# A conditioned two-stage block on one core: three bias matmuls, the order of the opening's loads and the order of VectorE's statistics are changed

## The chip, the cores and the metric

One of the eight NeuronCores of a Trainium2 chip (trn2) runs the kernel. The metric is device time in microseconds (us) of one launch. All arithmetic that matters here is float32; every float32 matmul goes through TensorE in two passes, which is why the profile counts two instructions for each matmul of the program.

## The reference

x is 32 batches of 128 tokens with 512 features; `cond` is 32 x 512; the mask is 32 x 128.

```python
emb = silu(t) @ ada_w + ada_b
shift, scale, gate_msa = split(emb, 3, axis=1)
norm = layernorm(x) * (1 + scale[:, None]) + shift[:, None]
norm = where(mask, norm, 0)
ssm_out = where(mask, (gelu(norm @ ssm_w1 + ssm_b1) @ ssm_w2 + ssm_b2)
                    + (gelu(norm @ bwd_w1 + bwd_b1) @ bwd_w2 + bwd_b2), 0)
x = x + gate_msa[:, None] * ssm_out
ff_ada = silu(t) @ ffada_w + ffada_b
shift, scale, gate = split(ff_ada, 3, axis=1)
ff_norm = layernorm(x) * (1 + scale[:, None]) + shift[:, None]
return x + gate[:, None] * (gelu_tanh(ff_norm @ ff_w1 + ff_b1) @ ff_w2 + ff_b2)
```

The first stage has an effect on masked tokens alone. The mask of these inputs marks the tail of a batch, up to 32 tokens.

## The kernel before

**Two stages.** The first stage gathers the masked tokens into 512 *slots*, four tiles of 128 (`xc[0]` to `xc[3]`). The slots' token numbers are counted from the mask with small matmuls (`slots_to_count`, L254) and compares on VectorE (`counted`). Tiles 0 and 1 are called early, tiles 2 and 3 late. Each tile is normalised, scaled and shifted (`modulated_by_strips`, L347 and L351), transposed by TensorE (`transposed_slots`, L193), copied by ScalarE (L196) and multiplied with `w1` (`hidden_of_tile` L673, `hidden` L204) and `w2` (`project`, L221). The result goes to DRAM (`x1_wide`, `x1_rows`), from where indirect gathers put the rows back in their places among the straight rows of x (`take_first_rows`, L813). The second stage runs over four pairs of two groups of four batches, and multiplies by a 7-product (Strassen) scheme: `FirstProduct` (L1118) and `SecondProduct` (L1305).

**Conditioning.** `mod1` (first stage) and `mod2` (second stage) hold shift, scale and gate. Matmuls of the transposed silu(cond) with `ada_a` or `ada_f` (`modulation_matmuls`, L309) add up in a PSUM bank. Before them the bank is filled with the bias by a matmul of `quarter`, a widened 4 x 4 identity, with `modb`, the bias rows (`modulation_bias`, L296). There are three such banks: `pm_ss` (shift and scale of stage one), `pm_g` (its gate) and `pm_f` (all three of stage two). VectorE copies each bank to SBUF (`modulation_rows`, L320). `of_slots` (L333) spreads the rows of `mod1` over the slots of a tile. The spread rows in PSUM are called strips (`part_s0` for tiles 0 and 1 together, `part_s2` for tiles 2 and 3).

**Order.** Almost everything stands under a manual schedule: each engine runs its instructions in the order of the program's text, and waits only on semaphores. All large loads go through SyncE's queue (SP), in order. They are, after `ada_a`'s first two thirds: `w1`'s first half (behind a one-element memset by GpSimd that holds it back until the first gather is issued), `ada_a`'s gate third, `w1`'s second half, `raw[0]`, `raw[1]`, `b2`, `b2b`, `w2`'s first half, `fw1` (2 MB), `w2`'s second half, `raw[2]`, `raw[3]`, `ada_f` (3 MB). `raw[n]` are the first eight batches of x, two in each tile of 512 KB.

**VectorE's order in the first stage**, after the early slots: the gate's rows; the statistics of `raw[0]` and `raw[1]` (`own_statistics`, L171), those of both late tiles, the strips of late tile 2, `b2 + b2b` (L792), the strips of late tile 3; the four combinations of `fw1` (`Weights.combine`, L394); the statistics of `raw[2]`; `finish_slots(0)` (L372 on), which ends with the store to `x1_wide`; the statistics of `raw[3]`; `weight_sums(3)` (L733); `finish_slots(1)`; the rows of `mod2` (L320); the normalised rows of the first four batches (L842), whose gathers read `x1_wide`.

On TensorE, the transposes of `mod2` (`ptr_mod`, L866) stand between the first and the second block of the late tiles' hidden layer, and everything behind them waits for `mod2`.

In the first pair (p == 0), at the change from the first to the second product, VectorE normalises and turns the rows of the next pair (`blocks(0, i)`, L929 and L1476) between the sums that the second product reads (`first_block`, L1252). When all four are turned, SP moves them with 16 transfers into `xT` (`to_feature_rows`, L956), ScalarE scales them (L939) and VectorE forms the sums of the next product (L986).

`keep_clock` (L620), L647 and `on_zeros` (L453) are matmuls whose result nobody reads.

Of the kernel before, what the change touches and what calls it, by code (L numbers as in the profile page):

```python
# [9 lines left out]
F32 = mybir.dt.float32  # L10
# [12 lines left out]
def kernel(  # L23
# [49 lines left out]
    nc = tc.nc  # L73
# [55 lines left out]
    def load_conditioning_bias(at, vec, queue):  # L129
        queue.dma_start(modb[at], vec.rearrange("(m j c) -> j m c", m=3, c=P))  # L130

    def load_blocks(t, w):
        nc.sync.dma_start(t, w.rearrange("(k p) f -> p k f", p=P))

    def load_behind_gathers(t, w):
        nc.gpsimd.memset(t[0:1, 0, 0:1], 0.0)
        load_blocks(t, w)

    modb = adap.tile([B + KC, 3, P], F32, name="modb")
    AT_A, AT_F = slice(0, KC), slice(B, B + KC)  # L140
    load_conditioning_bias(AT_A, ada_b, nc.sync)
# [47 lines left out]
    def transposed_slots(xn, dst, name):  # L189

        ptr = ps_t.tile([P, 512], F32, tag="tr", name=f"ptr_{name}")
        for k in range(KC):
            nc.tensor.transpose(ptr[:, ts(k, P)], xn[:, ts(k, P)], ident)  # L193
        for half_no in range(2):
            k = ts(half_no, KC // 2)
            nc.scalar.copy(dst[:, k], ptr.rearrange("p (k s) -> p k s", s=P)[:, k])  # L196
# [53 lines left out]
    def slots_to_count(picked, n, name, bank):  # L250

        pl = bank[0].tile([P, 512], F32, tag=bank[1], name=f"pl_{name}")
        for c in range(n):
            nc.tensor.matmul(pl[:, ts(c, S)], picked[:B, ts(c, P)], rank, start=True, stop=True)  # L254
        return pl[:, : n * S].rearrange("p (c s) -> p c s", s=S)
# [20 lines left out]
    def gather(dst, token_col):  # L276
        nc.gpsimd.indirect_dma_start(
            out=dst,
            out_offset=None,
            in_=x_rows,  # L280
            in_offset=bass.IndirectOffsetOnAxis(ap=token_col, axis=0),
        )
# [6 lines left out]
    def gather_slots(token_i):  # L289
        both = xp.tile([P, 2, D], F32, tag="x", name=f"xc_{len(xc)}")  # L290
        for c in range(NC // 2):
            gather(both[:, c], token_i[:, c : c + 1])
            xc.append(both[:, c])

    def modulation_bias(pm, at, lo, hi):
        nc.tensor.matmul(  # L296
            pm[:, : (hi - lo) * P],
            quarter[at],
            modb[at, lo:hi],
            start=True,  # L300
            stop=True,
            skip_group_check=True,
        )

    def modulation_matmuls(pm, ada, lo, hi, blocks):
        kinds = ada.rearrange("p k (m d) -> p k m d", d=D)
        for k in blocks:
            for j in range(KC):
                nc.tensor.matmul(  # L309
                    pm[ts(j, B), : (hi - lo) * P],  # L310
                    sT[:, k, :],
                    kinds[:, k, lo:hi, ts(j, P)],
                    start=False,
                    stop=True,
                    skip_group_check=True,
                )

    def modulation_rows(pm, mod, lo, hi):
        view = pm[:, : (hi - lo) * P].rearrange("p (m c) -> p m c", c=P)
        nc.vector.tensor_copy(mod[:, lo:hi], view)  # L320
# [130 lines left out]
    def on_zeros(*widths):  # L451
        for n in widths:
            nc.tensor.matmul(pm_keep_clock[:, :n], zeros[:, :P], zeros[:, :n], start=True, stop=True)  # L453
# [69 lines left out]
    def one_more_scale(at):  # L523
        nc.gpsimd.tensor_scalar(modb[at, 1], modb[at, 1], 1.0, None, ALU.add)

    one_more_scale(AT_A)
# [43 lines left out]
    quarter = adap.tile([B + KC, P], F32, name="quarter")  # L570
    for at in (AT_A, AT_F):
        nc.scalar.copy(
            quarter[at].rearrange("p (j b) -> p j b", b=B), ident[at, at].unsqueeze(2).to_broadcast([KC, KC, B])
        )
# [7 lines left out]
    load_conditioning_bias(AT_F, ffada_b, nc.scalar)  # L582

    both = xp.tile([P, 2, D], F32, tag="x", name="xc_0")
    for c, bank in enumerate(((ps_o, "o"), (ps_t, "tr"))):
        if c:
            on_zeros(256)
        slot = slot_col[:, c : c + 1]
        token_c = tokens_of(pick[:, ts(c, P)], slot, 1, f"s0_{c}", ssm, bank)
        xc.append(both[:, c])  # L590
        gather(xc[c], token_c)
        if c == 0:
            load_behind_gathers(w1[:, :, :D], ssm_w1)
    load_behind_gathers(ada_a[:, :, 2 * D :], ada_w[:, 2 * D :])
    load_blocks(w1[:, :, D:], bwd_w1)
    raw = [x_tile(2 * n, 2) for n in range(2 * G // 2)]
# [30 lines left out]

    pm = ps_o.tile([P, 512], F32, tag="o", name="pm_ss")
    modulation_bias(pm, AT_A, 0, 2)
    modulation_matmuls(pm, ada_a, 0, 2, range(KC))  # L630
    slots_of_late = slots_to_count(pick[:, NH:], NC // 2, "s1", (ps_h, "h"))
    modulation_rows(pm, mod1, 0, 2)

    strips = of_slots(pick, (0, 1), mod1, slice(0, 2), 3 * [(ps_o, "o")] + [(ps_h, "h")], "part_s0")
    keep_clock(2, 0)
# [4 lines left out]
    for c in range(2):  # L640
        mv, rstd = statistics(xc[c : c + 1], f"s{c}")
        xn_s.append(
            modulated_by_strips(xc[c], strips, c, xn[:, c], mv[:, 0, 0:1], rstd, xn[:, 2 + c])
        )
        if c == 0:
            for n in range(2):
                nc.tensor.matmul(  # L647
                    pm_keep_clock[:, ts(n, 2 * P)], ident, xn[:, 2, ts(n, 2 * P)], start=True, stop=True
                )
            token_i = counted(slots_of_late, slot_col[:, NC // 2 :], NC // 2, "s1", ssm)  # L650
    gather_slots(token_i)
    one_more_scale(AT_F)
# [4 lines left out]
    fb2 = const.tile([P, D], F32, name="fb2")  # L657
    load_blocks(fw1, ff_w1)
    load_blocks(w2[:, KC:], bwd_w2)
# [22 lines left out]
    transposed_slots(xn_s[0], xT_s[:, :, ts(0, P)], "s0")  # L682
# [10 lines left out]
    modulation_bias(pm, AT_A, 2, 3)  # L693
    modulation_matmuls(pm, ada_a, 2, 3, range(KC))
    modulation_rows(pm, mod1, 2, 3)
# [82 lines left out]
    for n in range(2):  # L778
        own_statistics(raw[n], 2, f"x_{n}")
    mv_t, rstd_t = statistics(xc[2:], "s23")  # L780
# [4 lines left out]
    for c in range(2):  # L785
        xn_late.append(
            modulated_by_strips(
                xc[2 + c], strips, c, spare[1][:, c], mv_t[:, c, 0:1], rstd_t[:, c : c + 1]
            )
        )  # L790
        if c == 0:
            nc.vector.tensor_tensor(b2, b2, b2b, ALU.add)  # L792
# [7 lines left out]
    own_statistics(raw[2], 2, "x_2")  # L800
# [31 lines left out]
    modulation_bias(pm, AT_F, 0, 3)  # L832
# [21 lines left out]
    modulation_rows(pm, mod2, 0, 3)  # L854
# [574 lines left out]
    for p in range(NP):  # L1429
# [78 lines left out]
        if more_pairs:  # L1508
            blocks(0, 2)
        second.step(1, late=True)  # L1510
        now.do(4, "P4")
        if more_pairs:
            blocks(0, 3)
            to_feature_rows(0, nc.sync)
        second.load_gate(1)
        second.first_block(1, 0, 2)
        second.seed_and_second_block(0)
# [172 lines left out]
```

## Time and profile before

| | us |
|---|---|
| three timed runs | 454.81, 454.75, 453.96 (median 454.75) |
| the profiled execution's own time | 454.21 |
| its span on the core | 452.5 |
| TensorE busy | 445.4 (98%) |
| VectorE busy | 334.2 (74%) |
| ScalarE busy | 178.5 (39%) |
| GpSimd busy | 158.0 (35%) |

The profile is of one execution on the chip. Times count from the start of the span. PE is TensorE, PEld its weight loads, DVE VectorE, ACT ScalarE, POOL GpSimd, SP SyncE; SPq marks a DMA issue. "L296" is line 296 of the kernel before. In the timeline a line has start, duration, engine, line, operation, output and input, how many are merged, and in brackets the idle time of the engine ahead of it and what ended it. In the chain of work a line has start, length and what. The chain gives each instruction the time from the end of its predecessor, the timeline its full duration.

### The profile page before, as it was taken

The page shows a single profiled execution, that of the slowest core. Times are in us where ns is not written, and L with a number is a line of the kernel's source. Part 1 is how long each engine was busy: PE and PEld are TensorE (multiplying, and loading weights), DVE is VectorE, ACT ScalarE, POOL GpSimd, SP SyncE. Part 2 cuts the span into 40 slices and gives each one's busy share as a digit, 9 for nine tenths or more (in the row PEclk, how much of TensorE's full clock was granted, in tenths as well). Part 3 has the DMA queues.
Part 4 walks back from the last instruction along what each step waited for, and adds up shares of the span by engine and source line. Part 5 has one row for each costly group of instructions (what it writes and reads, how often), then busy time and mean ns, then how long its engine had stood idle before and what let it go on. Part 6 is the DMA issues. An engine that isn't in the chain of part 4 may idle for free.

```text
span 452.5 us, 6201 instructions
## 1 busy us (share of the span) xinstructions
PE 445.4 (98%) x2151; PEld 370.6 (82%) x2151; DVE 334.2 (74%) x571; ACT 178.5 (39%) x390; POOL 158.0 (35%) x154
## 2 busy tenths in 40 slices
PE   8999999999999999999999999999999999999995
PEld 3885585688888888888888888888888888888884
DVE  5798797877799759987895598868964995434645
ACT  3124127253642551546425524464255144642000
POOL 4220550089770000797700007977000027560000
PEclk9999999999999999999999999999999999999999
DMA  7999449757327817741277177412771434122022
GB/s 254 376 395 408 152 72 332 246 186 236 123 98 159 115 49 257 245 138 36 89 172 112 48 251 245 141 38 90 167 106 58 175 128 129 35 94 93 0 92 98
DMA packets 84916, 70.58 MB, mean 156 GB/s; under 512 B 63368, under 2 KB 63984, under 8 KB 83858
## 3 DMA queue, kind: packets, MB, share of 16 engines
q1 hardware_dynamic: 70066, 58.28, 42.0%
q0 software_dynamic: 4160, 10.54, 6.8%
q10 hardware_dynamic: 10656, 1.33, 2.1%
q8 instruction: 18, 0.29, 0.3%
q14 instruction: 16, 0.13, 0.1%
HBM read 56.46 MB, written 13.70 MB: 155 GB/s over the span
## 4 chain that ended last, share of the span: by engine, by line
PE 94%; DVE 3%; POOL 1%; ACT 1%; issue 1%
PE a_o L1305 22%; PE a_m L1118 20%; PE e_o L1305 18%; PE e_m L1118 15%; PE po_s L221 6%; PE ph_s L204 5%; PE ph_s L673 2%; PE pm_ss L309 1%; PE last L1305 1%; PE a_m_alone L1118 1%; PE pm_f L309 1%; DVE s L1252 1%; PE pl_s L254 1%; PE part_s L333 0%; DVE xn L929 0%
## 5 line engine op out<-in xcount | busy, mean ns | idle before, releaser
L1169 POOL TENSOR_TENSOR ha<-p_m,ha 128x512 f32<-128x512 f32 x20 | 25.8, 1291 | 179.6 <-ACT ha L1176 169.7
L1305 PE MATMUL e_o<-fw,ha 128*128 128x256 f32 x256 | 57.9, 379 | 0.0
L939 ACT ACTIVATE xT<-xT,modT 128x128 f32<-128x128 f32 x112 | 44.2, 480 | 31.8 <-DMA xT<-xn 30.2
L1305 PE MATMUL a_o<-t,hb 128*128 128x256 f32 x240 | 54.1, 379 | 0.0
L1305 PEld LDWEIGHTS e_o<-fw,ha 128*128 128x128 f32 x256 | 48.6, 190 | 6.6
L1305 PEld LDWEIGHTS a_o<-t,hb 128*128 128x128 f32 x240 | 45.6, 190 | 6.2
L1080 ACT ACTIVATE hb<-hb,biasT 128x256 f32<-128x256 f32 x64 | 29.0, 500 | 29.5 <-POOL hb L1202 16.1
L1132 ACT COPY p_m<-e_m 128x512 f32<-128x512 f32 x27 | 15.8, 586 | 48.3 <-PE e_m L1118 44.2
L1305 PE MATMUL e_o<-fw,s 128*128 128x256 f32 x128 | 29.0, 380 | 0.6 <-DVE s L1252 0.6
L885 POOL DMA_INDIRECT x<-x_rows,slot_i x24 | 27.2, 1135 | 6.2 <-issue 5.4
L1169 POOL TENSOR_TENSOR hb<-p_m,hb 128x512 f32<-128x512 f32 x20 | 29.2, 1458 | 0.3
L1305 PE MATMUL a_o<-fw,ha 128*128 128x256 f32 x128 | 28.9, 379 | 0.0
L1305 PE MATMUL a_o<-t,s 128*128 128x256 f32 x128 | 28.9, 379 | 0.0
L221 PE MATMUL po_s<-w,h_s 128*128 128x512 f32 x64 | 28.4, 594 | 0.0
L1176 ACT COPY ha<-e_m 128x512 f32<-128x512 f32 x32 | 18.6, 580 | 24.8 <-PE e_m L1118 20.6
L1305 PEld LDWEIGHTS e_o<-fw,s 128*128 128x128 f32 x128 | 24.2, 190 | 4.3 <-DVE s L1252 1.0
L1305 PEld LDWEIGHTS a_o<-fw,ha 128*128 128x128 f32 x128 | 24.3, 190 | 3.3
L1305 PEld LDWEIGHTS a_o<-t,s 128*128 128x128 f32 x128 | 24.3, 190 | 3.3
L1143 DVE TENSOR_TENSOR e_m<-a_m,ha 128x512 f32<-128x512 f32 x20 | 14.0, 698 | 17.0 <-POOL ha L1169 7.6
L1080 ACT ACTIVATE ha<-e_m,biasT 128x256 f32<-128x256 f32 x48 | 20.1, 469 | 14.4 <-PE e_m L1118 14.2
L1118 PE MATMUL a_m<-xT,tw 128*128 128x256 f32 x96 | 24.7, 380 | 0.0
L1118 PE MATMUL e_m<-s,fw 128*128 128x256 f32 x92 | 23.7, 380 | 0.0
(237 smaller groups left out, 895.0 us busy)
## 6 DMA issues: line engine op xcount, KB each, us to landing
x<-in_x_dram SPq DMA_DIRECT2D x16, 512.0 KB
tw<-t_rows SPq DMA_DIRECT2D x16, 512.0 KB
gate<-gate_rows POOLq DMA_DIRECT2D x8, 1024.0 KB
out_dram<-x SPq DMA_DIRECT2D x15, 512.0 KB
tw<-t_rows SPq DMA_DIRECT2D x16, 384.0 KB
xT<-xn SPq DMA_DIRECT2D x92, 64.0 KB
ada_f<-in_L_cond_ffada_w_dram SPq DMA_DIRECT2D x4, 768.0 KB
ada_a<-in_L_cond_ada_w_dram SPq DMA_DIRECT2D x4, 512.0 KB
```

The source lines that it names most:

```text
L204: nc.tensor.matmul(ph[:, :n], w[:, k, ts(f, P)], xT[:, k, :], start=(k == 0), stop=(k == KC - 1))
L221: nc.tensor.matmul(po, h[f][:, ts(i, P)], w[:, f, :], start=(f == 0 and seeded is None), stop=(f == HC - 1), skip_group_check=seeded is no ...
L309: nc.tensor.matmul(pm[ts(j, B), : (hi - lo) * P], sT[:, k, :], kinds[:, k, lo:hi, ts(j, P)], start=False, stop=True, skip_group_check=True,)
L885: nc.gpsimd.indirect_dma_start(out=xs[i // G][i % G // 2][:, i % 2], out_offset=None, in_=x1_rows, in_offset=bass.IndirectOffsetOnAxis(ap= ...
L939: nc.scalar.activation(out, src, AF.Identity, bias=shift, scale=scale)
L1080: nc.scalar.activation(dst[:, n], src[:, n], AF.Gelu_apprx_tanh, bias=biasT[:, f : f + 1])
L1118: nc.tensor.matmul(bank[:, ts(n, QT)], self.w_block(j, product)[:, ts(n, P)], self.x_block(j, product), start=(product in ("P1", "P5") and ...
L1132: nc.scalar.copy(p5, e)
L1143: nc.vector.tensor_tensor(e, a, p5, add)
L1169: nc.gpsimd.tensor_tensor(self.place(RESULT[j], c), self.p5[j], other, ALU.add)
L1176: nc.scalar.copy(self.place(RESULT[j], c), src)
L1305: nc.tensor.matmul(part, src[:, k, ts(i, P)], w[product][:, k, :], start=(last and k == 0), stop=True, skip_group_check=True,)
```

## The change

1. The bias of the gate and of the second conditioning is no longer a matmul. It is loaded in broadcast form (each bias row to 32 partitions, 512 bytes a piece: `ada_b`'s gate part on SP behind `w1`'s second half, all of `ffada_b` on SP behind `ada_f` instead of on ScalarE's queue), and added by VectorE when it takes the rows out of PSUM: one `tensor_tensor`, and for the scale a `scalar_tensor_tensor` that also adds the 1.
2. The bias of `pm_ss` stays a matmul, but stands ahead of the second counting matmul, in place of a filler. ScalarE instead of VectorE copies `pm_ss` out.
3. In the opening, tile 0's strips are made alone (4 matmuls instead of 8) and tile 1's after tile 0's transposes. The second late counting matmul goes behind tile 0's strips. Fillers are halved. Tile 0's transposes go to two PSUM banks, so that ScalarE's first copy can start after two of them.
4. The gather of late tile 2 is issued ahead of tile 1's statistics, the one of tile 3 right behind them.
5. `ssm_w1` is loaded in two column halves (1 KB instead of 2 KB a piece). `w2`'s second half goes ahead of `fw1` on SP.
6. VectorE's order: `raw[0]`, then late tile 2 whole, late tile 3 whole, `b2 + b2b`, `raw[1]`, `raw[2]`, and only then the combinations of `fw1`.
7. In the first pair, `blocks(0, 2)` and `blocks(0, 3)` with the transfers to `xT` move behind `second.load_gate(1)`, the one around and the other behind `first_block(1, 0, 2)`.

```diff
-    def load_conditioning_bias(at, vec, queue):
-        queue.dma_start(modb[at], vec.rearrange("(m j c) -> j m c", m=3, c=P))
+    def load_conditioning_bias(t, vec, kinds):
+        rows = vec.rearrange("(m j c) -> m j c", m=3, c=P)
+        for n, m in enumerate(kinds):
+            nc.sync.dma_start(t[:, n], rows[m].unsqueeze(1).to_broadcast([KC, B, P]))
...
-    def transposed_slots(xn, dst, name):
+    def transposed_slots(xn, dst, name, apart=False):
+        ptr = [ps_t.tile([P, 512], F32, tag="tr", name=f"ptr_{name}")]
+        if apart:
+            ptr.append(ps_t.tile([P, 512], F32, tag="tr", name=f"ptr_{name}_1"))
...
-    def modulation_rows(pm, mod, lo, hi):
+    def modulation_rows(pm, mod, lo, hi, bias=None):
         view = pm[:, : (hi - lo) * P].rearrange("p (m c) -> p m c", c=P)
-        nc.vector.tensor_copy(mod[:, lo:hi], view)
+        if bias is None:
+            nc.vector.tensor_copy(mod[:, lo:hi], view)
+            return
+        other = slice(0, hi - lo, 2)
+        nc.vector.tensor_tensor(mod[:, lo:hi][:, other], view[:, other], bias[:, other], ALU.add)
+        if lo <= 1 < hi:
+            nc.vector.scalar_tensor_tensor(
+                mod[:, 1], view[:, 1 - lo], 1.0, bias[:, 1 - lo], ALU.add, ALU.add)
...
     for c, bank in enumerate(((ps_o, "o"), (ps_t, "tr"))):
         if c:
-            on_zeros(256)
+            modulation_bias(pm)
...
         if c == 0:
-            load_behind_gathers(w1[:, :, :D], ssm_w1)
+            load_behind_gathers(w1[:, :, : D // 2], ssm_w1[:, : D // 2])
+            load_blocks(w1[:, :, D // 2 : D], ssm_w1[:, D // 2 :])
     load_behind_gathers(ada_a[:, :, 2 * D :], ada_w[:, 2 * D :])
     load_blocks(w1[:, :, D:], bwd_w1)
+    load_conditioning_bias(modb[:, 2:], ada_b, (2,))
...
-    modulation_rows(pm, mod1, 0, 2)
-    strips = of_slots(pick, (0, 1), mod1, slice(0, 2), ..., "part_s0")
-    keep_clock(2, 0)
+    nc.scalar.copy(mod1[:, 0:2], pm.rearrange("p (m c) -> p m c", c=P)[:, 0:2])
+    slots_of_late = slots_to_count(pick[:, NH:], NC // 2, "s1", (ps_h, "h"), lambda: parts_of_tile(0))
+    keep_clock(1, 0)
...
+    modulated_slots(0)
+    nc.tensor.matmul(pm_keep_clock[:, : 2 * P], ident, xn[:, 2, : 2 * P], start=True, stop=True)
+    transposed_slots(xn_s[0], xT_s[:, :, ts(0, P)], "s0", True)
+    parts_of_tile(1)
+    token_i = counted(slots_of_late, slot_col[:, NC // 2 :], NC // 2, "s1", ssm)
+    late_slots()
+    gather(xc[2], token_i[:, 0:1])
+    modulated_slots(1)
+    gather(xc[3], token_i[:, 1:2])
...
+    load_blocks(w2[:, KC:], bwd_w2)
     load_blocks(fw1, ff_w1)
-    load_blocks(w2[:, KC:], bwd_w2)
     load_raw(2)
...
-    modulation_bias(pm, AT_A, 2, 3)
     modulation_matmuls(pm, ada_a, 2, 3, range(KC))
-    modulation_rows(pm, mod1, 2, 3)
+    modulation_rows(pm, mod1, 2, 3, modb[:, 2:])
+    load_conditioning_bias(modb, ffada_b, range(3))
...
-    for n in range(2):
-        own_statistics(raw[n], 2, f"x_{n}")
-    mv_t, rstd_t = statistics(xc[2:], "s23")
...
     for c in range(2):
+        if c == 0:
+            own_statistics(raw[0], 2, "x_0")
+        mv, rstd = statistics(xc[2 + c : 3 + c], f"s{2 + c}")
...
-        if c == 0:
-            nc.vector.tensor_tensor(b2, b2, b2b, ALU.add)
+    nc.vector.tensor_tensor(b2, b2, b2b, ALU.add)
+    for n in range(1, 3):
+        own_statistics(raw[n], 2, f"x_{n}")
...
     fw1_of.combine(0, 1, 2, 3)
-    own_statistics(raw[2], 2, "x_2")
...
-    modulation_bias(pm, AT_F, 0, 3)
     modulation_matmuls(pm, ada_f, 0, 3, range(KC))
...
-    modulation_rows(pm, mod2, 0, 3)
+    modulation_rows(pm, mod2, 0, 3, modb)
...
         second.first_block(1, 2, 4)
-        if more_pairs:
+        if more_pairs and p:
             blocks(0, 2)
         second.step(1, late=True)
         now.do(4, "P4")
-        if more_pairs:
+        if more_pairs and p:
             blocks(0, 3)
             to_feature_rows(0, nc.sync)
         second.load_gate(1)
+        if p == 0:
+            blocks(0, 2)
         second.first_block(1, 0, 2)
+        if p == 0:
+            blocks(0, 3)
+            to_feature_rows(0, nc.sync)
         second.seed_and_second_block(0)
```

## The prediction

> **What bounds the kernel now.** I read the page's busy times, then the chain of waits, then VectorE's timeline and the busy time by stage.
>
> ```profile
> span 452.5 us, 6201 instructions
> ...
> PE 445.4 (98%) x2151; PEld 370.6 (82%) x2151; DVE 334.2 (74%) x571; ACT 178.5 (39%) x390; POOL 158.0 (35%) x154
> ...
> PE 94%; DVE 3%; POOL 1%; ACT 1%; issue 1%
> ```
>
> TensorE is the bound. The chain shows where it does work that the change takes away, and two places where it reads what VectorE makes (L866, L945):
>
> ```profile
> 7.69 3.57 PE pm_ss L309 x32
> 11.27 0.81 PE pl_s L254 x3
> 12.08 0.98 PE part_s L333 x14
> ...
> 16.15 3.81 PE ph_s L673 x32
> ...
> 20.39 0.41 PE pm_g L296 x2
> ...
> 49.99 0.84 PE pm_f L296 x2
> ...
> 55.47 0.22 PE ptr_mod L866 x2
> ...
> 67.78 0.44 PE ptr L945 x4
> ```
>
> TensorE's waits after the opening come to one:
>
> ```profile
> PE e_o L1305 <- DVE s L1252: 0.6, 1, 0.6
> ```
>
> So a shorter TensorE list is worth its length as long as VectorE keeps up. Its timeline, from the first weight combination on:
>
> ```profile
> 34.77 1.22 DVE L394 TENSOR_TENSOR t<-fw 128x1024 f32<-128x1024 f32 x1 [0.86 <-DMA fw<-in_L_cond_ff_w_dram]
> ...
> 39.69 0.69 DVE L171 BATCH_NORM_STATS2 st_x<-x 128x6 f32<-128x512 f32 x1
> ...
> 42.36 0.69 DVE L372 TENSOR_TENSOR t_s<-po_s,gs 128x512 f32<-128x512 f32 x1 [0.76 <-PE po_s L221]
> ...
> 49.15 0.69 DVE L372 TENSOR_TENSOR t_s<-po_s,gs 128x512 f32<-128x512 f32 x1 [0.36 <-PE po_s L221]
> ...
> 53.61 0.56 DVE L320 COPY mod<-pm_f 128x384 f32<-128x384 f32 x1 [1.91 <-PE pm_f L309]
> 54.34 0.55 DVE L842 TENSOR_SCALAR xn<-x 128x512 f32<-128x512 f32 x1 [0.17 <-DMA x<-x_wide,slot_i]
> ```
>
> Its idle time from 34 to 54 us is 0.86 + 0.76 + 0.36 + 1.91, or 3.9 us, and the first of it ends with a load. The loads run without a gap (columns: busy us and count of PE, PEld, DVE, ACT, POOL, then clock, DMA share, GB/s):
>
> ```profile
> 20.00:30.00 10.00, 10.00 (x104) 8.66 (x103) 7.56 (x30) 2.80 (x7) 2.92 (x5) 1.00 1.05 392
> 30.00:40.00 10.00, 10.00 (x63) 6.50 (x62) 9.04 (x19) 4.97 (x10) 0.00 (x0) 1.00 1.03 398
> ```
>
> **What TensorE gains up to ptr_mod.** *Opening.* pm_ss's end (11.27) stays: its last block of ada_a lands at 10.15 (0.62 us of idle before it), whatever stands in front. The bias matmul there (0.85) takes the place of a filler (0.33), so the second token, gather and pick come some 0.5 later. Tile 1's rows are read at 16.14 with no wait; I take 0, at worst 0.5. ScalarE's copy of 128x256 takes 0.33 (L196: 0.65 for two) against VectorE's 0.42, and VectorE's statistics (0.68) no longer stand behind it. Four strips instead of eight cost 8 passes of 0.07 instead of 16: 0.5 less before tile 0 can start, so the first strip product moves from 13.10 to about 12.45. Transposes in two banks let ScalarE copy 0.3 earlier; tile 1's strips (0.5) then lie in front of L673 and hide the copies and the 0.27 of "issue" there. L673 starts near 15.6 instead of 16.15: 0.55. *Bias matmuls.* Both pieces lie on the chain: 0.41 and 0.84. The gate's add replaces a copy of the same 128x128 (0.29). Its broadcast bias (64 KB) is queued behind w1, which is read at 26.8, and needed at 21: by the queue's order it is there. Together 1.8: TensorE is ready for ptr_mod at 53.67 instead of 55.47.
>
> The earlier late gathers and the order of strips let VectorE finish tile 3's strips earlier: one pair's statistics (1.81: 23.67 to 25.48) and b2's sum (0.61) leave the stretch ahead of them, which ended at 33.9, exactly when gate_s wanted their banks. Without that, the 0.96 that TensorE has gained by then would be lost in a wait there; it brings no more than that. w2's second half 2 MB sooner does the same for po_s at 36.9.
>
> **What VectorE loses.** raw[2]'s statistics now stand in front of the combinations of fw1, and raw[2] is behind fw1 in the queue. In the row fw1 has landed at 34.7; behind it come w2's half (1.05 MB) and raw[2] (0.52 MB) at 395 GB/s: 2.66 + 1.33, so raw[2] lands at 38.7. The change does not alter what is ahead of raw[2], apart from two additions: the gate's bias, 64 KB or 0.17, and ssm_w1 in 1 KB pieces. For these the page's queues give a price: q10's 10656 packets of 125 bytes hold 2.1% of 16 x 452.5 us, 14 ns each; q0's 4160 of 2.5 KB hold 6.8%, 118 ns. On the line between them 1 KB takes 53 ns and 2 KB 97, so 1024 against 512 packets cost 4.6 us of engine time, 0.3 on 16 engines. Bounds 0 and 0.6; I take 0.3. raw[2] is there at 39.2, and VectorE, done with raw[1] near 34, waits 5 us for it.
>
> [...]
>
> From 39.2 on VectorE has, by starts of rows: raw[2] 1.90 (39.69 to 41.59), combinations 4.92 (34.77 to 39.69), finish_slots(0) 2.47 (42.36 to 44.83), raw[3] 1.80, weight sums 2.16 (46.63 to 48.79), finish_slots(1) 2.55 (49.15 to 51.70), and mod2's rows, now an add of 128x256 (0.42, like L320's copy) and one of 128x128 (0.34, like L347 after PSUM), 0.7 after overlap. Sum 16.5: mod2 is ready at 55.75, with the release to TensorE 55.85. TensorE stands at ptr_mod from 53.67: a stall of 2.2, and it goes on 0.4 later than before. The whole 1.8 is eaten, because nothing on TensorE's list between can be moved ahead. Bounds: raw[2] 0.8 sooner or 0.7 later move this one for one.
>
> [...]
>
> *Behind ptr_mod.* finish_slots(0) starts at 46.1 instead of 42.36, so x1_wide's store goes from 45.63 to 49.4 and the first gather from 49.52 to 51.8 (if the store lands faster on a queue that is empty by then) or 53.2. L842 came 4.8 after that gather while weight sums were stored beside it; the later ones take less. First normalised rows: 55.9 to 58; I take 56.5, or 2.2 later. VectorE has no idle from 54.34 to the end of the last normalised rows at 65.44: that becomes 67.6, and L945 (67.61 + 0.4) can just start. Nothing more is lost here, but the 2.2 us of slack are gone.
>
> *First pair.* Two blocks of 1.2 (133.39 to 134.60, 135.18 to 136.37) leave the path to first_block: it can end near 135.9, and TensorE, done with P1V at 136.45, loses its 0.63 of wait. But the transfers to xT start at 137.05 instead of 136.54 and carry ScalarE's scaling, for which VectorE waited 5.5 us at 165.05. From there VectorE has no idle until 182.28. Its seed at 180.62 then ends 0.5 later while TensorE comes 0.63 sooner: of the slack there (181.32 to 182.08) 0.35 is missing, and at 185.50 (slack 0.2) up to 0.95. Bounds -0.63 and +0.35; nearest is the seed's row, -0.28; I take -0.2.
>
> ptr_mod +0.4, first pair -0.2: +0.2. The profiled execution's 454.21 becomes 454.4. It lies 0.54 below the median of the three runs (454.75), so the forecast for a median is 455.0.
>
> **Rivals.** *Faster: VectorE keeps up.* If raw[2] has landed by 37.1, no stall appears at ptr_mod; 1.8 and some 0.3 of the first pair stay, which gives 452.7; halfway (38.0) about 453.6. For it: VectorE's work is the same as before and it had 3.9 idle. Against it: 20 to 40 us run at a DMA share of 1.03 to 1.05, and the order on SP puts fw1 ahead. Chance 0.24.
>
> *Slower: the rows' way through DRAM.* x1_wide's store, gather and normalised rows are 2.2 to 3.7 late. From 57.0 on for the first L842, L945 waits too, one for one; at 58.0 to 58.8 that is 1.0 to 1.8 on top of the 0.4, and if the first pair gives nothing back, 456.2 to 457.0. For it: the row shows 3.9 from store to gather and 4.8 to the rows. Against it: the queue was still busy with ada_f then. Chance 0.20.
>
> *The bias matmuls were hidden anyway* would give the same time by another way; the chain, with both pieces in it, speaks against.
>
> **Numbers.** The forecast's case has 0.56, with a range of its own from 454.0 to 456.1; of it 0.36 lie within 0.2% (0.9 us, about what a measurement of this kernel can tell from no change) and 0.20 above. With the rivals: faster 0.24, same 0.36, slower 0.40. For 8 in 10 the range reaches to half of the faster case and most of the slower: 452.9 to 456.7.
>
> **What would show it.** Right: L673 starts near 15.6; L296 is gone from pm_g and pm_f; VectorE idles about 5 us for x before raw[2]'s statistics, at 34 to 39; the chain goes over VectorE ahead of ptr_mod, near 55.9, with some 2 us of TensorE's wait; the wait at 137 is gone, and TensorE waits for VectorE once or twice between 180 and 187. Wrong: ptr_mod before 54.5, or raw[2]'s statistics starting before 38; or a new wait before 34, at gate_s or for a weight.

## The result and the profile after

The changed kernel takes 456.4 us (median of 16 executions, 454.48 to 458.19), the kernel before 454.37 beside it (16 executions, 453.96 to 454.97). The ratio is 1.0036, with a 95% interval from 1.0023 to 1.005: slower by 0.36%. The executions now spread over 3.7 us instead of 1.0. In all ranges and ratios here, four single executions in a far slower state (668 to 1207 us) are left out.

The profiled execution is one of the quickest, 454.56. The page's head, TensorE's busy time and the shares of the chain that ended last:

```profile
span 452.8 us, 6181 instructions
...
PE 445.6 (98%) x2136; PEld 369.8 (82%) x2136; DVE 333.8 (74%) x572; ACT 178.4 (39%) x390; POOL 159.6 (35%) x154
...
PE 73%; DVE 9%; DMA 6%; SPq 5%; ACT 2%; issue 2%; POOL 1%; ACTq 0%
```

TensorE's list is shorter, and still its share of the chain fell from 94% to 73%: DMA, SP's queue and VectorE now set the end over a long stretch. The chain of waits leads through raw[2]'s load and VectorE's list up to ptr_mod. Start, length, what:

```profile
23.34 15.84 DMA x<-in_x_dram
...
39.20 0.70 DVE st_x L172
...
54.84 0.43 DVE mod L328
...
55.32 0.53 PE ptr_mod L882 x2
55.85 4.32 PE ph_s L208 x20
```

As forecast, VectorE stands 4.5 us idle ahead of raw[2]'s statistics, and ptr_mod waits for mod2. VectorE's timeline, with the bracket for the idle time ahead:

```profile
39.20 0.69 DVE L172 BATCH_NORM_STATS2 st_x<-x 128x6 f32<-128x512 f32 x1 [4.50 <-DMA x<-in_x_dram]
...
56.70 0.78 DVE L858 TENSOR_SCALAR xn<-x 128x512 f32<-128x512 f32 x1 [1.23 <-DMA x<-x_wide,slot_i]
```

This execution is only 0.35 us above the profiled one of before, so it does not show where the median's 2.0 us are. For that another execution was wanted.

### The profile page after: what moved, and what is told of

Read it like the earlier page. It is cut to its first block, busy times and chain, and to the rows that moved or that the text cites. A ratio compares the mean times of both kernels' runs of the same rounds, so it can differ in the third digit from the quotient of the medians.

```text
span 452.8 us, 6181 instructions
## 1 busy us (share of the span) xinstructions
PE 445.6 (98%) x2136; PEld 369.8 (82%) x2136; DVE 333.8 (74%) x572; ACT 178.4 (39%) x390; POOL 159.6 (35%) x154
## 4 chain that ended last, share of the span: by engine, by line
PE 73%; DVE 9%; DMA 6%; SPq 5%; ACT 2%; issue 2%; POOL 1%; ACTq 0%
PE a_m L1134 19%; PE a_o L1321 18%; PE e_m L1134 15%; PE e_o L1321 14%; SPq L972 4%; DMA x<-in_x_dram 3%; PE po_s L225 3%; PE ph_s L208 3%; DMA w<-in_L_cond_bwd_w_dram 2%; ACT xT L955 1%; SPq L135 1%; PE last L1321 1%; PE a_m_alone L1134 1%; DVE fw L408 1%; DVE t_o L1295 1%
## 5 line engine op out<-in xcount | busy, mean ns | idle before, releaser
L225 PE MATMUL po_s<-w,h_s 128*128 128x512 f32 x64 | 28.4, 594 | 0.0
L1134 PE MATMUL a_m<-xT,tw 128*128 128x256 f32 x96 | 24.7, 380 | 0.0
L1134 PE MATMUL e_m<-s,fw 128*128 128x256 f32 x92 | 23.9, 382 | 0.1
```

The source lines that it names most:

```text
L225: nc.tensor.matmul(po, h[f][:, ts(i, P)], w[:, f, :], start=(f == 0 and seeded is None), stop=(f == HC - 1), skip_group_check=seeded is no ...
L1134: nc.tensor.matmul(bank[:, ts(n, QT)], self.w_block(j, product)[:, ts(n, P)], self.x_block(j, product), start=(product in ("P1", "P5") and ...
```

## The experiments

Line numbers are those of the changed kernel, unless another is named. "Before" in a comparison is the kernel before, run beside the experiment on the same chip (medians 454.44 to 454.61).

### The changed kernel once more

No edit.

> The changed kernel once more, on the chip and beside the runs that the next three share. Its 16 executions ran from 454.48 to 458.19 with a median of 456.4, while the kernel before stayed within 453.96 to 454.97; the profiled one was the 454.56. All theories expect a median near 456.4 again. What is wanted is a profile of a high execution. Clock theory (TensorE's own clock falls in some executions, because the opening has fewer filler matmuls and more pauses): the extra 2 to 3 us stand in one stretch before 30 us, in matmuls of the same form that take up to twice as long, with no new wait. VectorE theory (raw[2] ahead of fw1's combinations): they stand in TensorE's wait at ptr_mod, 0.62 in the low execution, and grow there. Pair theory (transfers to xT 0.9 later): they stand between 165 and 190 us as TensorE's waits for VectorE.

Measured: 456.37 (455.58 to 457.19), ratio 1.0039 [1.0027, 1.0051]. The profile caught an execution of 456.45. TensorE's waits in it:

```profile
PE ptr_mod L882 <- DVE mod L328: 1.7, 1, 1.7
...
PE a_m L1134 <- DVE hb L1164: 0.5, 1, 0.5
PE ptr L961 <- DVE xn L858: 0.4, 1, 0.4
```

The wait at ptr_mod grew to 1.7, as the VectorE theory said, but a second wait follows at L961, the *turn*: there TensorE transposes the normalised rows of the second four batches (`xn_0_1`), which read both stores to x1_wide. The chain of waits says where that one comes from:

```profile
24.91 15.15 DMA x<-in_x_dram
40.08 0.71 DVE st_x L172
...
46.81 0.69 DVE t_s L386
...
53.24 0.61 DVE t_s L386
...
56.86 0.59 POOL t_s L176
...
64.97 3.83 DMA x<-x_wide,slot_i
68.83 0.56 DVE xn L858
69.38 0.04 issue
69.43 0.33 PE ptr L961
69.76 1.72 PE po_s L225 x4
```

ptr_mod is not in this chain. It runs from raw[2]'s landing over VectorE to finish_slots, over GpSimd's small step L176 to the second store to x1_wide, over the gathers to the eighth batch, the last of the second four, and only then to TensorE. Before, VectorE normalised these four at its own pace (first line); here it waits for the last of them:

```profile
63.53 1.91 DVE L842 TENSOR_SCALAR xn<-x 128x512 f32<-128x512 f32 x4
```

```profile
66.71 1.45 DVE L858 TENSOR_SCALAR xn<-x 128x512 f32<-128x512 f32 x3
68.83 0.55 DVE L858 TENSOR_SCALAR xn<-x 128x512 f32<-128x512 f32 x1 [0.67 <-DMA x<-x_wide,slot_i]
```

The blocks of po_s behind the turn start at 69.59, where the kernel before has 68.05: 1.54 of the 2.2 us between the two spans. Both ways are late: ptr_mod alone ends at 56.65 instead of 55.68, so without the eighth batch the turn would still have been 0.97 late. Another 0.50 is the wait of L1134, at 295 us.

The opening tells the opposite of the clock theory as it was put. TensorE's timeline of the first, quicker execution:

```profile
11.75 1.23 PE L347 MATMUL part_s<-mod,pick 32*128 32x256 f32 x8
12.76 0.63 PE L260 MATMUL pl_s<-rank,pick 32*128 32x128 f32 x2
13.32 1.08 PE L632 MATMUL pm_keep_clock<-ada_a,sT 128*32 128x256 f32 x8
14.33 1.22 PE L665 MATMUL pm_keep_clock<-xn_s,ident 128*128 128x256 f32 x2
```

and of this, slower one:

```profile
11.45 0.71 PE L347 MATMUL part_s<-mod,pick 32*128 32x256 f32 x8
11.99 0.38 PE L260 MATMUL pl_s<-rank,pick 32*128 32x128 f32 x2
12.30 0.64 PE L632 MATMUL pm_keep_clock<-ada_a,sT 128*32 128x256 f32 x8
12.87 0.70 PE L665 MATMUL pm_keep_clock<-xn_s,ident 128*128 128x256 f32 x2
```

From start to start the eight passes of `keep_clock` (L632) take 1.01 in the first and 0.57 in the second. The half speed in the opening is real, but it stands in the quick execution: the first hidden product starts at 16.75 there and at 15.37 in the slow one. It is not what makes this execution slow.

### raw[2]'s statistics behind fw1's combinations again

```diff
-    for n in range(1, 3):
-        own_statistics(raw[n], 2, f"x_{n}")
+    own_statistics(raw[1], 2, "x_1")
...
     fw1_of.combine(0, 1, 2, 3)
+    own_statistics(raw[2], 2, "x_2")
```

> The changed kernel with raw[2]'s statistics put back behind fw1's combinations. VectorE theory: VectorE idles some 0.5 us rather than 4.5 at 34.7, the wait of 0.62 at ptr_mod goes, ptr_mod starts near 54.7, the median falls by 0.6 or more (all of the 2.0 lost, if the high executions wait longer there), and the spread of 3.7 us shrinks. Clock theory: at most the 0.6 of the low execution; the median stays at 455.8 or above and the spread stays near 3.7. Pair theory: no more than 0.6 either.

Measured: 454.46 (453.63 to 456.74), ratio 1.0 [0.9988, 1.0012]: 1.9 below the run of the change beside it. The wait at ptr_mod is gone, and that at L961 is 0.20. VectorE still stands idle for 3.0 us, now for fw1, because w2's half is ahead of it in the queue:

```profile
37.76 1.23 DVE L408 TENSOR_TENSOR t<-fw 128x1024 f32<-128x1024 f32 x1 [2.96 <-DMA fw<-in_L_cond_ff_w_dram]
...
54.65 0.38 PE L882 MATMUL ptr_mod<-ident,mod 128*128 128x128 f32 x2
```

One step of VectorE's order carries the whole loss of the median. The spread, which the VectorE theory had shrinking, stays at 3.1 us.

### The fillers of the opening restored

```diff
+            on_zeros(256)
             modulation_bias(pm)
...
-    keep_clock(1, 0)
+    keep_clock(2, 0)
...
-    nc.tensor.matmul(pm_keep_clock[:, : 2 * P], ident, xn[:, 2, : 2 * P], start=True, stop=True)
+    for n in range(2):
+        nc.tensor.matmul(
+            pm_keep_clock[:, ts(n, 2 * P)], ident, xn[:, 2, ts(n, 2 * P)], start=True, stop=True
+        )
```

> The changed kernel with the fillers of the opening as they were before: the matmul on zeros ahead of the second token beside the bias, two rounds of the clock-keeping matmuls, and two of those on the modulated rows. Its list is longer by about 0.33 + 0.5 + 0.5 us if the clock is full. Clock theory: tile 0's passes take 0.07 each and not 0.14, the first hidden product starts no later than 16.75 although the list is longer, the spread between executions falls to about 1 us as before the change, and the median falls by 1.5 to 2 us to 454.4 to 454.9. VectorE theory: the median stays near 456.4 (up to 0.5 later or nothing, since ptr_mod waits for VectorE anyway). Pair theory: stays too.

Measured: 455.45 (455.11 to 458.19), ratio 1.003 [1.0014, 1.0047], whose interval overlaps that of the change. The passes of part_s run at 0.07 and the first hidden product starts at 15.96, but the spread stays at 3 us, where the clock theory had about 1, and ptr_mod waits 1.8. Nine of the twelve executions lie within 0.7 us (455.11 to 455.79), the other three at 456.77 to 458.19. So the opening's half speed is not all of the spread; a gain of up to 0.9 is left possible.

### The first pair's blocks in their former places

```diff
-        if more_pairs and p:
+        if more_pairs:
             blocks(0, 2)
...
-        if more_pairs and p:
+        if more_pairs:
             blocks(0, 3)
             to_feature_rows(0, nc.sync)
         second.load_gate(1)
-        if p == 0:
-            blocks(0, 2)
         second.first_block(1, 0, 2)
-        if p == 0:
-            blocks(0, 3)
-            to_feature_rows(0, nc.sync)
```

> The changed kernel with the first pair's blocks and transfers in their former places. Pair theory: the wait of 0.6 at 137 us comes back, those of 0.2 to 0.3 at 180, 182 and 186 go, and the median falls by 1 us or more, with the spread. Clock theory and VectorE theory: the same within 0.3 us, spread near 3.7.

Measured: 456.16 (455.46 to 457.94), ratio 1.004 [1.0025, 1.0054]. TensorE's wait of 0.63 for `first_block` is back, and the time is the same. The pair theory fell as the cause of the loss.

This profile shows another loss. From ptr_mod to the turn TensorE has the same 56 passes as in the profiled execution of the change, and needs 1.6 us more for them. Chain of waits, the change and here:

```profile
55.85 12.16 PE ph_s L208 x56
```

```profile
55.71 13.77 PE ph_s L208 x56
```

The busy time by stage says why: behind the wait of 2.02 us at ptr_mod the granted clock (third column from the end) falls. One stretch before and here:

```profile
57.00:58.00 1.00, 1.00 (x6) 0.87 (x6) 1.00 (x3) 0.47 (x1) 0.69 (x2) 1.00 0.03 0
```

```profile
57.00:58.00 1.00, 1.00 (x4) 0.81 (x3) 0.97 (x3) 0.00 (x0) 0.95 (x1) 0.50 0.65 255
```

Microsecond by microsecond from 55 to 60 it reads 0.90, 0.50, 0.50, 0.50 and 0.89, so about 3.4 us at half clock. There is no wait for rows at the turn here; TensorE itself comes at 69.32. In the profiles of the change, of its repetition and of fillers, with waits of 0.6, 1.75 and 1.77 at ptr_mod, the 56 passes behind it take 12.32, 12.25 and 12.29 in the timeline, against 13.94 here; in the change's the clock reads 1.00 in each of these microseconds.

### mod2's rows ahead of finish_slots(1)

```diff
-    store_rows.append(finish_slots(1, project(1, h1, w2, "s1", seeded=po_s[1]), gs[1]))
-    for i in range(2, 2 * G):
-        take_first_rows(i)
+    po_1 = project(1, h1, w2, "s1", seeded=po_s[1])
...
     modulation_rows(pm, mod2, 0, 3, modb)
+    store_rows.append(finish_slots(1, po_1, gs[1]))
+    for i in range(2, 2 * G):
+        take_first_rows(i)
```

> The changed kernel with VectorE's rows of mod2 put ahead of finish_slots(1), so that TensorE's wait at ptr_mod goes (1.7 and 2.0 us in the repeated run and in the one with the first pair as before) while the second store of x1_wide leaves no sooner, rather 0.7 us later. Theory of the stall at ptr_mod: that wait is the loss, the median falls by 1.5 us or more from 456.3, to 454.8 or below. Theory of the rows' way through DRAM (second store of x1_wide, its gathers, normalised rows, turn at L961 of the changed kernel): ptr_mod starts by 54.5 without a wait, but the last normalised rows of the first four still come near 69 and TensorE waits there for what it saved, so that the median stays within 0.5 of 456.3, or goes to 457.

Measured: 456.4 (454.91 to 457.18), ratio 1.0032 [1.0019, 1.0045]: no change against the changed kernel. ptr_mod starts without a wait for VectorE, and TensorE waits at the turn instead:

```profile
55.87 0.38 PE L883 MATMUL ptr_mod<-ident,mod 128*128 128x128 f32 x2
...
69.69 0.33 PE L962 MATMUL ptr<-ident,xn 128*128 128x128 f32 x1 [1.13 <-DVE xn L856]
70.49 0.33 PE L962 MATMUL ptr<-ident,xn 128*128 128x128 f32 x1 [0.47 <-DVE xn L856]
```

So the wait at ptr_mod can go without any gain. It does not separate the two ways fully, since the edit itself makes the second store later (58.22, against 56.06 and 57.47 in the two profiles of the change) and so pays at the turn for what it saves. (In this execution the half speed lasted up to the hidden products: tile 1's part_s took 1.24 against 0.71 in the repetition. They started at 17.57, so ptr_mod is late for that reason.)

### raw[2] and the order of the weights undone

```diff
-    load_blocks(w2[:, KC:], bwd_w2)
     load_blocks(fw1, ff_w1)
+    load_blocks(w2[:, KC:], bwd_w2)
```

on top of the edit for raw[2].

> The changed kernel with two of its moves undone: raw[2]'s statistics behind fw1's combinations, and w2's second half behind fw1 in SP's queue (fw1 landed 3.0 us later than before where only the first was undone). VectorE theory, with the rows' way behind it: combinations start near 34.8 again, finish_slots(1) ends by 52, the gathers leave as early as before the change, and what TensorE saves up to ptr_mod (1.25 us of bias matmuls, up to 0.9 of the opening) stays: median 452.5 to 453.6, 0.9 to 2 below 454.46. Theory that the weights' order does not matter once raw[2] is back: 454.3 to 454.6 again. If po_s waits for w2's half, up to 0.7 of it is lost.

Measured: 454.89 (454.51 to 456.17), ratio 1.0005 [0.9995, 1.0015]. The expectation of a gain failed. The first store to x1_wide leaves at 45.93 as before the change, but the first gather behind it starts at 52.38. GpSimd's timeline before the change (L813) and here (L830):

```profile
49.52 1.15 POOL L813 DMA_INDIRECT x<-x_wide,slot_i  x1 [1.65 <-DMA x_wide<-t_s]
```

```profile
52.38 1.08 POOL L830 DMA_INDIRECT x<-x_wide,slot_i  x1 [4.20 <-DMA x_wide<-t_s]
```

### The same with the first pair undone as well

The diffs of order_back and of pair_back together.

> As order_back, and the first pair's blocks and transfers in their former places as well. With nothing late ahead of the first pair, this shows what that part is worth: by the prediction it gains 0.2 (bounds -0.63 and +0.35), so this kernel is 0.2 above order_back; by the pair theory (transfers to xT 0.9 later make VectorE late at 180 to 187) it is 0.3 or more below it.

Measured: 455.05 (454.15 to 455.85), ratio 1.0011 [1.0002, 1.002]. It is 0.16 above order_back, with overlapping intervals. The first pair's part is worth nothing that these runs can tell, either way.

### The bias by VectorE alone

The kernel before with `load_conditioning_bias`, `modulation_rows`, `modulation_matmuls` and `quarter` of the changed kernel, the gate's rows loaded behind `w1`, those of the second conditioning behind `ada_f`:

```diff
-    modulation_bias(pm, AT_A, 2, 3)
...
-    modulation_rows(pm, mod1, 2, 3)
+    modulation_rows(pm, mod1, 2, 3, modb[:, 2:])
+    load_conditioning_bias(modb, ffada_b, range(3))
...
-    modulation_bias(pm, AT_F, 0, 3)
...
-    modulation_rows(pm, mod2, 0, 3)
+    modulation_rows(pm, mod2, 0, 3, modb)
```

> The kernel before with one part of the change alone: the bias of gate and second conditioning added by VectorE, its rows loaded in the changed kernel's places of SP's queue; opening, order of loads, raw[2] and first pair as before. By the prediction's terms TensorE's list is shorter by 0.41 + 0.84 = 1.25 and VectorE had 1.91 us of idle ahead of mod2's rows: ptr_mod starts near 54.3 rather than 55.47 and the median is 453.2 to 453.6. If the rows' way through DRAM binds behind ptr_mod anyway, TensorE waits at L945 instead and the median stays at 454.4; if the rows of the bias in SP's queue delay raw[2] or the weights, it is slower than before.

Measured: 453.97 (453.63 to 454.41), ratio 0.9988 [0.9979, 0.9997]: the one version whose interval lies below the kernel before, by 0.5 us, where 0.85 to 1.25 had been expected. In its profile the first store leaves at 45.96, the first gather waits for its landing as in order_back, and VectorE waits for the rows of the eighth batch:

```profile
51.90 1.08 POOL L819 DMA_INDIRECT x<-x_wide,slot_i  x1 [3.70 <-DMA x_wide<-t_s]
```

```profile
66.96 0.55 DVE L847 TENSOR_SCALAR xn<-x 128x512 f32<-128x512 f32 x1 [1.07 <-DMA x<-x_wide,slot_i]
```

So it uses up the slack ahead of the turn, and its bias loads are suspect. But the turn itself lost little: TensorE reached ptr_mod only 0.50 sooner than before (54.80 against 55.30) and waited under 0.2 at the turn. Most of what is missing went earlier, at gate_s, which needs the banks of tile 3's strips from VectorE. VectorE's last strips and the first po_s behind gate_s, before and here:

```profile
32.80 1.11 DVE L351 SCALAR_TENSOR_TENSOR x<-x,rstd_s,part_s 128x128 f32<-128x128 f32 x4
...
35.11 5.42 PE L221 MATMUL po_s<-w,h_s 128*128 128x512 f32 x12
```

```profile
33.12 1.12 DVE L362 SCALAR_TENSOR_TENSOR x<-x,rstd_s,part_s 128x128 f32<-128x128 f32 x4
...
35.44 4.99 PE L222 MATMUL po_s<-w,h_s 128*128 128x512 f32 x11
```

In both, and in loads_only and bias_early too, po_s starts 1.20 after VectorE's last strip ends. VectorE is 0.33 later here (why is open), so the 0.41 of pm_g saved ahead of it cannot count, and of pm_f's 0.84 there remain 0.5.

### The loads of the bias alone

The kernel before with three loads added, which nothing reads:

```diff
+    rows = ffada_b.rearrange("(m j c) -> m j c", m=3, c=P)
+    for m in range(3):
+        nc.sync.dma_start(spare[0][:, 0, ts(m, P)], rows[m].unsqueeze(1).to_broadcast([KC, B, P]))
```

> The kernel before, with only the three loads of the second conditioning's bias in rows (3 x 64 KB, each piece 512 bytes, by SP behind ada_f) added to it, into a tile that is not read then; its matmuls of bias stay. Theory of the loads: in bias_only and order_back the first store of x1_wide left at 45.9 as before, but the first gather waited until 51.9 and 52.4 (49.5 before), because these pieces crawl beside it at 80 to 200 GB/s; so here too the first gather starts near 52, the second store leaves near 55 rather than 52.6, and of the slack before L945 (about 2.2 us) most is gone: the median rises by 0 to 0.7 from 454.45. Rival (what delays the gather is that the stores are earlier or TensorE's list is shorter): the first gather stays at 49.5 to 50, median the same within 0.2.

Measured: 454.34 (454.18 to 455.06), ratio 1.0001 [0.9992, 1.001]. The store leaves at 45.67, and

```profile
51.22 1.15 POOL L816 DMA_INDIRECT x<-x_wide,slot_i  x1 [3.31 <-DMA x_wide<-t_s]
...
53.71 0.58 POOL L175 TENSOR_TENSOR t_s<-t_s,half 128x1 f32<-128x1 f32 x1
```

the first gather starts 1.7 later than before although nothing else was changed. GpSimd's step for the second store (L175) stands behind the first two gathers in its queue and comes at 53.71 instead of 52.01, so the second store leaves at 54.31 instead of 52.61. The time does not move: the kernel before has room for it. The busy time by stage, one stretch before and here (last two columns: DMA share, GB/s), shows the queue still at work where it had been empty:

```profile
48.00:49.00 1.00, 1.00 (x4) 0.38 (x3) 0.79 (x1) 0.00 (x0) 0.00 (x0) 1.00 0.00 0
```

```profile
48.00:49.00 1.00, 1.00 (x4) 0.34 (x3) 0.82 (x1) 0.00 (x0) 0.00 (x0) 1.00 0.22 70
```

### The loads ahead of ada_f

bias_only with

```diff
-    load_conditioning_bias(modb, ffada_b, range(3))
...
+    modb_g = adap.tile([P, 1, P], F32, name="modb_g")
+    load_conditioning_bias(modb, ffada_b, range(2))
+    load_conditioning_bias(modb_g, ffada_b, (2,))
     load_ada(ada_f, ffada_w, range(KC), 3 * D)
```

> bias_only with these three loads ahead of ada_f in SP's queue (the third into a tile of its own; the rows of mod2 in three VectorE instructions instead of two). Theory of the loads: the first gather is back at 49.5 to 50.3, the last normalised rows of the first four no longer wait for x, ptr_mod starts near 54.5 and the turn follows without a wait; the 1.25 us of bias matmuls come through for 0.9 to 1.2, median 453.2 to 453.6 against 453.97 of bias_only. Rival: the rows' way stays as late and the median stays near 453.97, or ada_f comes too late for pm_f and it is worse.

Measured: 454.96 (454.54 to 455.32), ratio 1.0011 [1.0002, 1.002]: 1.0 worse than bias_only. The cure failed. The loads hold SP's queue from 29.37 to 37.0, ada_f is issued from 37.12 instead of 28.96, and now it is ada_f that stands in front of the store (DMA share 1.02 to 1.05 from 44 to 47 us): the first gather starts at 52.76, and TensorE waits 0.52 at the turn. ScalarE's queue, where the one load stood before the change, was not tried.

### The same in the changed kernel, without and with fillers

order_back with the last diff, and then with that of the fillers as well.

> order_back with the three loads ahead of ada_f as in bias_early, so the changed kernel's opening, late slots, bias by VectorE and first pair are in, raw[2], fw1 and the second conditioning's loads are not. Theory of the loads: the median falls from 454.89 by 1 us or more, to 453.0 to 453.8, with the spread that the opening's clock gives (first hidden product at 15.3 or at 16.8). If raw[2] and the weights' order were all of it, it stays at 454.5 to 455.

> order_early with the former number of fillers in the opening. The profiles so far show the first hidden product at 15.2 to 15.4 (three) or 16.7 to 17.6 (four) without them, and at 16.0 to 16.7 with them. Clock theory: the first hidden product starts near 16, part_s passes take 0.07 each, the spread of the executions narrows, and the median lies within 0.4 of order_early's, since the fillers cost about what the slow clock costs on average. If the fillers were not needed it is 0.5 to 0.8 slower.

Measured: 455.91 (455.56 to 457.24), ratio 1.0036 [1.0024, 1.0049], and with fillers 455.55 (454.56 to 455.77), ratio 1.0024 [1.0014, 1.0033]. The same fault, plus a wait of TensorE for w2's second half (1.18 us at po_s without fillers, 0.33 with them). The faster opening only runs into it sooner.

## Why the prediction was right or wrong

The forecast was 455.0 in 452.9 to 456.7, slower by over 0.2% the likeliest of the three. The median, 456.4, lies in the range, but it is the slower rival's case (456.2 to 457.0, chance 0.20) and not the forecast's own (454.0 to 456.1). That the range holds it is owed to the rival and not to the sum, which came to 455.0.

The way of the rows in the profiled executions. Stores and gather from the timelines of SP and GpSimd; the last column is the first block of po_s behind the turn (L225; L221 and L222 in kernels made from before):

| kernel | own time | first store | first gather | second store | po_s behind the turn |
|---|---|---|---|---|---|
| before | 454.21 | 45.63 | 49.52 | 52.61 | 68.05 |
| change | 454.56 | 49.20 | 53.03 | 56.06 | 68.38 |
| change, again | 456.45 | 50.08 | 54.14 | 57.47 | 69.59 |
| mod2_first | 456.83 | 48.92 | 53.15 | 58.22 | 70.65 |
| pair_back | 456.31 | 49.13 | 53.10 | 56.52 | 69.76 |
| raw2_behind | 453.77 | 47.76 | 51.97 | 55.15 | 67.81 |
| fillers | 455.27 | 49.66 | 54.10 | 57.12 | 68.85 |
| order_back | 455.60 | 45.93 | 52.38 | 55.59 | 68.44 |
| order_pair_back | 454.93 | 45.87 | 52.61 | 55.85 | 68.73 |
| bias_only | 453.87 | 45.96 | 51.90 | 54.92 | 67.73 |
| loads_only | 454.34 | 45.67 | 51.22 | 54.31 | 68.09 |
| bias_early | 454.54 | 46.09 | 52.76 | 56.05 | 68.40 |
| order_early | 456.21 | 45.80 | 53.49 | 56.66 | 69.58 |
| order_early_fillers | 455.34 | 45.28 | 53.01 | 56.21 | 69.18 |

The last column plus 386 us is the own time within 0.3 in nine of the fourteen (added: 386.0 to 386.3). The others are fillers (386.4), order_early (386.6), pair_back (386.6), again (386.9) and order_back (387.2), which lose up to 1 us more behind the turn. Part of it is waits of TensorE for VectorE: 0.50 at 295 us in again, 0.31 there in pair_back, 0.21 at 175 and 0.51 at 294 in order_back, 0.21 at 176 in order_early. What makes them come and go is open.

Step by step:

- *Bias matmuls, 0.41 and 0.84.* Right for TensorE's list: L296 is gone from both pieces of the chain, and alone the edit gains 0.5 us. That it is not 1.25 is shown by bias_only's profile for that execution: VectorE's strips ahead of gate_s set po_s, as the prediction had said of the old order, and took the 0.41 and 0.33 of the rest, and the turn took 0.2. What the prediction left out of its sum are the edit's DMAs. It costed the gate's rows in the queue and not the three loads of the second conditioning, which make the first gather 1.7 later (loads_only); that cost the time nothing there, and in bias_only no more than the 0.2 at the turn. Within the whole change they cost little, because the store leaves 3.6 later there and finds them gone (gather 3.8 behind the store, as before).
- *raw[2] at 39.2, VectorE idle 5, ptr_mod 2.2 late.* Right in size: 38.92 to 40.08 in five profiles, idle 2.9 to 4.7, and waits at ptr_mod of 0.6, 1.7, 1.8 and 2.0.
- *"Nothing more is lost here" behind ptr_mod.* This step failed. The prediction took the first normalised rows as the measure (56.5 forecast; 56.49 to 57.52 measured) and let the later ones follow at VectorE's pace. In the profiled execution that nearly holds: no wait of 0.2 or more at the turn, and po_s 0.33 late, near the forecast's 0.4. In the repeated one po_s is 1.54 late, 0.97 of it by ptr_mod and the rest by the rows of the eighth batch. (The expectations call these the last of the first four; it is the eighth gather, issued at 64.97, that they wait for.) They hang on the second store, which leaves 3.0 to 3.4 behind the first gather in every row of the table but mod2_first's, because GpSimd's L176 stands behind two gathers in its queue; VectorE has the rows 11 to 12.3 us after that store (57.47 to 68.83 in the repeated run). The first rows are no measure of this: in order_back they come at 54.99, and the turn still waits 0.88. The rival had this way and its size, with the wrong rows as its threshold.
- *The granted clock.* The sum has no term for a fall of it. It falls: in pair_back's profile the granted clock is 0.50 for about 3.4 us, and the hidden products take 1.6 longer. The wait ahead of it was 2.02. Whole executions point the same way. (A mean of 0.997 or 0.998 occurs in all kernels, bias_only's profiled execution of 453.87 among them. Behind the last matmul, from 448 us on, the clock reads 0.96 in the profile of before and 0.98 in the change's, against 1.00 from 440 to 448; a fall there costs nothing.) A mean granted clock of 0.996 or less, an estimated 1.8 us lost over 455 us if TensorE is at work meanwhile, stands in 4 of the change's 16 executions, 2 of 7 of pair_back and 1 of 12 of fillers, all seven between 456.31 and 458.19. It stands in none of the 6 of the repetition, none of the 90 of the other experiments and none of the 81 of the kernel before that ran beside them. Without its four, the change's other twelve have a median of 455.8. That the wait at ptr_mod brings the fall about fits this, but no run isolates it.
- *The place of the loss.* raw2_behind shows it: with raw[2] back behind the combinations the median falls by 1.9. How the loss divides between ptr_mod, the rows and the clock differs between the profiles, and is open for the median. mod2_first shows that taking the wait at ptr_mod away does not bring the time back when the rows come no sooner.
- *Opening, L673 near 15.6.* It is 15.1 to 15.4 in four profiles without the old fillers and 16.75 to 17.6 in four others. In the first four, where the passes go over to 0.07 before 12 us, the part gains 0.8 to 1.1, more than the 0.55 of the sum; in the others it loses 0.6 to 1.4. The term that failed is "8 passes of 0.07": in the profiled execution they took nearly twice that (0.126). The profile's row of the granted clock shows 9 throughout. In the slow stretch, 11.75 to 15.35, TensorE was busy all through, and the longest pause ahead of it, past the first 2 us, was 0.21. What divides the executions into the two groups is open. TensorE was ready for ptr_mod 0.6 to 2.1 us earlier than before, against the 1.8 of the sum (change 0.60, again 0.92, fillers 1.37, pair_back 2.13); again also shows a wait of 0.20 at gate_s, which the prediction had named as a sign of being wrong. The time did not follow any of these, since ptr_mod or the turn waited.
- *First pair, -0.2.* The wait at 137 went and came back as forecast (0.63), and the time showed neither (456.37 against 456.16, 454.89 against 455.05). The waits forecast between 180 and 187 came too: in the change's profile L1134's blocks at 180.15, 182.08 and 186.63 start 0.24, 0.10 and 0.14 later than 0.86 after the block ahead, the pace of the others, and so give most of the 0.63 back.
- *The median 0.54 above the profiled execution.* This failed too: the spread grew with the change, and the median lies 1.8 above. Before, TensorE's own list reached the turn last (67.61, without a wait) and took no notice of when a gather landed; in the change ptr_mod takes a delay of raw[2]'s landing, and the turn one of a gather. That fits the wider spread, and so does the clock; no run isolates either.

## What to carry to other kernels

Follow a moved step through every queue that its result passes, to the last consumer in front of which the bound engine stands, and not to the first: here one statistics step on VectorE delayed a store, a GpSimd step behind two gathers, and the last of eight gathers. A wait on the bound engine is no price until the next wait behind it has been checked, nor is a saving one until the next wait behind it has been (pm_g's 0.41 ended at gate_s). Look at the granted clock behind a new wait, in more than one execution (0.50 behind one of 2.02 us in pair_back, 1.00 behind one of 0.62 in the change). An edit that swaps a matmul for a broadcast has DMAs to be priced as well (three loads here made the first gather 1.7 later); and when a change eats the slack of a path through DRAM, look at the spread as well as the median (here 3.7 us instead of 1.0, and 2.0 later).

## What was unexpected of the hardware

Small matmuls of the opening ran at half speed (0.126 against 0.063 to 0.07 us from pass to pass) for about 3.6 us (11.75 to 15.35) while the granted clock read 1.00 and TensorE was busy without a gap. Another execution of the same kernel ran the same matmuls at full speed (0.07).

The granted clock fell to 0.50 for about 3.4 us right behind a wait of TensorE of 2.02 us (pair_back); behind waits of 1.75 (again) and 1.77 (fillers) the same 56 passes were not slowed (12.25 and 12.29 us, against 13.94).

Three loads of 64 KB in pieces of 512 bytes (beside 58.28 MB on their queue, q1, in the page of before) added 1.7 us to the time from a 257 KB store, issued 2.4 us after the issue of the last of them ended, to the gather that waits for it (3.89 became 5.55, loads_only). Moving them ahead of the large load did not help, since SP then issued that load 8 us later (37.12 instead of 28.96, bias_early).
